# A Mamba block between two graph layers: where the first two chunks' convolutions and heads keep their accumulators, when the second head runs, and when activation tables are called for

## The chip, the cores and the metric

The kernel runs on one core of a Trainium2 chip. The metric is the device time of one execution in microseconds (us); of several executions the median is taken. The engines of a core work at the same time, each through its own queue in order: TensorE (PE in the profile; its weight loads are PEld), VectorE (DVE), ScalarE (ACT), GpSimd (POOL) and SyncE (SP, which here only issues DMA transfers). Matrix products land in PSUM, which this kernel divides into eight banks of 128 x 512 float32; everything else lies in SBUF.

## The reference, cut to what matters

Four graph layers follow each other on 3327 nodes with 256 features, each with a residual sum and a layer norm around it. Layer 1 is the one that the change touches: a graph convolution, then a Mamba block over the nodes as a sequence.

```
h = relu(adj @ x @ gcn_w + gcn_b)
h = (h - mu) * rsqrt(var + eps) * ln_g + ln_b
# _mamba(h):
xz = h @ w_in                      # 256 -> 2 * 512
xc, z = xz[:, :512], xz[:, 512:]
xconv = sum(xpad[k:k + L] * conv_w[:, k] for k in range(4)) + conv_b
u = silu(xconv)
dbc = u @ w_xp                     # 512 -> 16 + 16 + 16
dt = softplus(dbc[:, :16] @ w_dt + b_dt)
B, C = dbc[:, 16:32], dbc[:, 32:]
dA = exp(dt[:, :, None] * A[None]);  dBu = dt[:, :, None] * B[:, None, :] * u[:, :, None]
hst = dA_t * hst + dBu_t           # a scan over the nodes, 16 states a channel
y = (hst @ C_t) + u * D_skip
return (y * silu(z)) @ w_out
```

Softplus is computed as max(v, 0) + log(1 + exp(-|v|)) with a correction for rounding.

## The kernel before

The 3327 nodes are padded to 26 tiles of 128. Layer 0 comes first, TensorE alone being busy. Layer 1 follows, and its sequence is cut into seven **chunks**: one of 256 nodes (tiles 0 and 1), then six of 512 (four tiles each). Layers 2 and 3 come after it and are not touched.

**Graph convolution.** `convolve()` (L308) is a generator that yields after every few matmuls. For each tile it multiplies 26 blocks of the adjacency matrix, fetched in three transfers of up to nine blocks into two buffers (L318, L319), with the features, into `acc`, one half of a PSUM tile `cb` (L313). Then the tile's **evacuation** follows: ACT copies it (L328), PE transposes it into the other half `tp` (L331), ACT copies again (L333), PE multiplies with `gcn_w` into `acc` (L336, L337), and ACT takes relu out of it (L340), which is the last read of `cb`. ACT and POOL then make the layer norm (L298 to L306, L347), PE transposes (L357) and ACT writes the tile into `hT` (L359), the input of Mamba. Each unit of work has a count: 122 a tile (`TILE`), 96 of them for the matmuls of 24 blocks.

**A head** (class `Head`, L460) prepares one chunk: `project(g)` for the four groups g of 128 channels (two matmuls, then on ACT a copy and the first tap, L474 to L477); `taps(g)`, three multiply-adds on DVE (L484); `silu` (ACT); `mixed`, the product with `w_xp` and its copy to `left` (L498 to L500), from which B and C also go to DRAM (L503); `step_size(g)`, a small matmul and two ACT operations (L512 to L514); `exponentials(g)` for two groups at a time (ACT Exp of `e`, then `e1 = 1 + e`); `rounding` (DVE, L526), `logarithms` (ACT Ln of `e1`), `finish` (three DVE operations, L534 to L537; `e1` is then dt, and `du` is dt times u) and `skip` (ACT multiplies u by D_skip). The big temporaries of the heads, `xc`, `left`, `v`, `e`, `e1`, come from `scratch()` (L199), a pool of four buffers of one tile name `t`. `e1` stays in use as dt for the whole chunk.

**The states.** A chunk is worked off in 16 **slots**, one for each state s. In a slot DVE does four scans (L586, one a group) and one product with C (L593, into one of two buffers `hc`), and POOL makes the scan's input for two slots later (`feed`, L580). ACT makes the decays dA (L572) into two PSUM buffers, each released by its scan. PE adds the product, transposed, to the accumulators `y0` to `y3` (`add_up`, L601; one bank for each tile of the chunk). The rows of B and C come by DMA on SP's queue (L569), into three buffers.

**Order.** The main loop runs over all 7 x 16 slots. In slot s of chunk c the steps of the head of chunk c + 1 are put where `plan(c)` says (L246), and convolution units for the chunk after that are spread over the slots: `quota` (L409) levels the counts of `duty` (L390) and adds 96 units (`AHEAD`) at the start. A scheduler then orders the instructions of PE and ACT by priority and by when it thinks operands are there; steps under `tc.high_priority()` go ahead, among them the sums of the first slots (L671: `s == 0 or k < 5`). In the loop (`pinned`) DVE and POOL keep the order in which the program was written, and steps called through `in_turn` (L279: decays, silu, exponentials, logarithms) keep theirs on ACT.

**Before the loop** tiles 0 and 1 are convolved (L635), the first head runs at high priority (L638), and tiles 2 to 5 are convolved (L652).

**PSUM.** The pools of layer 1 hold eight banks: `y0` to `y3`, one for each; `ps`, one for everything else of the heads, gates and residuals; two for dA; and one for `cb`. The first chunk has two tiles, so it uses `y0` and `y1` only, and `y2` and `y3` are first used when the second chunk begins.

Of the kernel before, what the change touches and what calls it, by code (L numbers as in the profile page):

```python
# [9 lines left out]
F32 = mybir.dt.float32  # L10
# [37 lines left out]
def gnn_kernel(ctx: ExitStack, tc: tile.TileContext, n: int, a: dict, out: bass.AP):  # L48
# [109 lines left out]
    with tc.tile_pool(name="l1b", bufs=1) as wpool, tc.tile_pool(name="l1at", bufs=2) as l1at:  # L158
# [33 lines left out]
        with tc.tile_pool(name="l1aw", bufs=1) as cwork, tc.tile_pool(name="l1c", bufs=2) as ch, \  # L192
# [53 lines left out]
            def plan(c):  # L246


                if c == 0:
                    return dict(project={g: (g,) for g in range(NG)}, taps={g + 2: (g,) for g in range(NG)}, gates={6: (0, 1)},  # L250
                                silu=5, mixed=7, sizes={g + 8: (g,) for g in range(NG)}, exps=(11, 12), log=13)
                return dict(project={5: (0, 1), 6: (2, 3)}, taps={7: (0, 1), 8: (2, 3)}, gates={7: (0, 1), 8: (2, 3)},
                            silu=8, mixed=9, sizes={9: (0,), 10: (1, 2), 11: (3,)}, exps=(11, 12), log=13)

# [35 lines left out]
                gps.tensor_scalar(rs, var, EPS, None, op0=ALU.add)  # L290
                gps.tensor_tensor(rs, rs, mhalf[:, :var.shape[1]], op=ALU.pow)

            def back_to_exp():
                in_turn(act.activation, small.tile([P, 1], F32, name="ex"), eps_t, AF.Exp)

            def spread(y, sm, nm, sq):

# [10 lines left out]
            def convolve():  # L308

                rest = []  # L310
                full = 0
                for it in range(nt):
                    cb = cpsum.tile([P, 2, D], F32, name="cb")  # L313
                    acc, tp = cb[:, 0, :], cb[:, 1, :]
                    for j in range(nt):
                        if j % JC == 0:
                            m = min(JC, nt - j)
                            at = l1at.tile([P, JC, P], F32, name="at")  # L318
                            nc.sync.dma_start(at[:, :m, :], a["adjT"][it][:, j:j + m, :])  # L319
                        ten.matmul(acc, at[:, j % JC, :], X0[:, j, :], start=(j == 0), stop=(j == nt - 1))  # L320
                        if j % JM == JM - 1 and j < nt - 1:
                            if rest:
                                step = rest.pop(0)
                                step()
                                full += step is turn
                            yield full, 4 * JM
                    m = cwork.tile([P, D], F32, name="m")
                    act.copy(m, acc)  # L328
                    yield full, 8
                    for k in range(2):  # L330
                        ten.transpose(tp[:, k * P:(k + 1) * P], m[:, k * P:(k + 1) * P], ident)  # L331
                    mt = cwork.tile([P, D], F32, name="m")
                    act.copy(mt, tp)  # L333
                    yield full, 4
                    for k in range(2):
                        ten.matmul(acc, mt[:, k * P:(k + 1) * P], gw[:, k, :], start=(k == 0), stop=False)  # L336
                    ten.matmul(acc, one, gb, start=False, stop=True)  # L337
                    h = cwork.tile([P, D], F32, name="hn")
                    rs, nb, nm, sm, sq = (small.tile([P, 1], F32, name=x) for x in ("rs", "nb", "nm", "sm", "sq"))
                    act.activation(h, acc, AF.Relu, accum_out=sm)  # L340
                    spread(h, sm, nm, sq)

                    def measure(rs=rs, nb=nb, nm=nm, sq=sq):
                        scales(rs, nb, nm, sq)

                    def norm(h=h, rs=rs, nb=nb):
                        turn_or_not = in_turn if pinned else lambda op, *x, **k: op(*x, **k)  # L347
                        turn_or_not(act.activation, h, h, AF.Identity, scale=rs, bias=nb)

                    def turn(it=it, h=h):  # L350
                        c = next(x for x in range(nch) if it * P < ends[x])
                        i = it * P - starts[c]
                        if i == 0:
                            hTs[c] = ch.tile([P, D // P, WC], F32, name="hT", bufs=3)
                        pt = psum.tile([P, WC], F32, name="ps")
                        for k in range(2):
                            ten.transpose(pt[:, k * P:(k + 1) * P], h[:, k * P:(k + 1) * P], ident)  # L357
                        for k in range(2):
                            act.activation(hTs[c][:, k, i:i + P], pt[:, k * P:(k + 1) * P], AF.Identity,  # L359
                                                 scale=g1[:, k:k + 1], bias=b1[:, k:k + 1])  # L360
                    rest = [*2 * [lambda: None], measure, *2 * [lambda: None], norm, lambda: None, turn]
                    if not pinned:
                        for step in (measure, norm, turn):
                            step()
                        rest = []
                        full += 1
                    yield full, 14
                for step in rest:
                    step()
                    full += step is turn  # L370
                    yield full, 0
# [88 lines left out]
            class Head:  # L460
# [4 lines left out]
                def project(self, g):  # L465

                    c, w = self.c, self.w
                    if g == 0:
                        self.xc = scratch()
                        gps.tensor_copy(self.xc[:, :, :3], last)  # L470
                        us[c] = ch.tile([P, NG, WC], F32, name="u", bufs=1)[:, :, :w]
                    ps = psum.tile([P, WC], F32, name="ps")
                    for k in range(2):
                        ten.matmul(ps[:, :w], w_in[:, k, g * P:(g + 1) * P], hTs[c][:, k, :w],  # L474
                                   start=(k == 0), stop=(k == 1))
                    act.copy(self.xc[:, g, 3:3 + w], ps[:, :w])
                    act.activation(us[c][:, g, :], self.xc[:, g, 0:w], AF.Identity, scale=conv_w[:, g, 0:1],  # L477
                                   bias=conv_b[:, g:g + 1])
# [13 lines left out]
                def mixed(self):  # L492

                    c, w = self.c, self.w
                    m = w_sp.shape[2]
                    ps = psum.tile([P, WC], F32, name="ps")
                    for g in range(NG):
                        ten.matmul(ps[:m, :w], w_sp[:, g, :], us[c][:, g, :], start=(g == 0), stop=(g == NG - 1))  # L498
                    self.left = scratch()[:m, 0, :w]
                    act.copy(self.left, ps[:m, :w])  # L500
                    bc = rows_of[c] = l1d.tile([2, DS, w], F32, name=f"bc{c}")
                    for k in range(2):
                        nc.sync.dma_start(bc[k], self.left[32 * k + DTR:32 * k + DTR + DS])  # L503

                def step_size(self, g):

                    w = self.w
                    if g == 0:
                        self.v, self.e = (scratch()[:, :, :w] for _ in range(2))
                    ps = psum.tile([P, WC], F32, name="ps")  # L510
                    k = slice(32 * g, 32 * g + DTR)
                    ten.matmul(ps[:, :w], w_dt[k, :P], self.left[k], start=True, stop=True)  # L512
                    act.activation(self.v[:, g, :], ps[:, :w], AF.Identity, bias=b_dt[:, g:g + 1])
# [63 lines left out]
                in_turn(act.activation, dA, dt[:, g, :], AF.Exp, scale=A[:, g, states[k][1]:states[k][1] + 1])  # L577
                return dA

            def feed(k):  # L580

                du = xs[states[k][0]][1]
                w = du.shape[2]
                gps.tensor_tensor(hs[k % 2][:, :, :w], du, rows[k][:, 0:1, :].to_broadcast([P, NG, w]), op=ALU.mult)

            def scan(k, g, dA):  # L586

# [23 lines left out]
            def gated(c, i):  # L611

                pt = psum.tile([P, NG, P], F32, name="ps")
                for g in range(NG):
                    ten.transpose(pt[:, g, :], szs[c][:, i, g * P:(g + 1) * P], ident)
                gt = tmp.tile([P, NG, P], F32, name="gt", bufs=1)
                act.copy(gt, pt)
                return gt

# [18 lines left out]
            with tc.high_priority():  # L638
                for g in range(NG):
                    first.project(g)  # L640
                    first.taps(g)
                first.silu()
                first.mixed()
                for g in range(NG):
                    first.step_size(g)
                for g in (0, 2):
                    first.exponentials(g)
                first.rounding()
                first.logarithms()
                first.finish()  # L650
                first.skip()
            pump(ends[1] // P)  # L652
            states = [(c, s) for c in range(nch) for s in range(DS)]
            rows = {k: row(k) for k in range(2)}
            for k in range(2):
                feed(k)
            dAs = [decay(0, g) for g in range(2)]
            pinned = True
            added = None
            turned = []  # L660
            for k, (c, s) in enumerate(states):
# [39 lines left out]
                    scales(plus[0], plus[1], plus[2], plus[4])  # L701
                if s == 14:
                    in_turn(act.activation, szs[c], szs[c], AF.Silu)
                    back_to_exp()
                if after:
                    if s == p["silu"]:
                        ahead.silu()
                        back_to_exp()
                    elif s == p["log"]:
                        ahead.logarithms()  # L710
                        back_to_exp()
                    elif s == 15:
                        ahead.skip()
                    if s in p["exps"]:
# [864 lines left out]
```

## Time and profile before

| | us |
|---|---|
| median of three runs (3562.14 to 3568.34) | 3562.71 |
| the profiled execution, whole | 3553.07 |
| its span, first to last instruction | 3551.3 |
| PE, DVE, ACT, POOL busy in the span | 3267.4, 2370.3, 1736.8, 931.8 |
| first matmul of the graph convolution (tile 0) | about 357 |
| first scan of chunk 0 | 428.1 |
| first scan of chunk 1 | 570.3 |
| last product of chunk 6 done | 1403.0 |

How to read the lines: a group of instructions is given as engine, line of the code, operation, output <- input, shape, and count; a bracket at the end says how long the engine was idle before it, and which engine and tile ended that. Lines at L274 are calls through the class that pins the order, and lines at L281 are calls through `in_turn`, so there one goes by the tile's name: `h<-dA` is a scan, `hc` a product, `u<-t` the taps, `dA` a decay, and `t<-t` exponentials or logarithms. A float32 matmul is recorded as two instructions. In a table of stretches of time, each line gives the stretch, its length, and then for each engine the busy time and the number of instructions in it, followed by the granted TensorE clock, the share of DMA time and GB/s.

### The profile page before, as it was taken

The page shows a single profiled execution, that of the slowest core. Times are in us where ns is not written, and L with a number is a line of the kernel's source. Part 1 is how long each engine was busy: PE and PEld are TensorE (multiplying, and loading weights), DVE is VectorE, ACT ScalarE, POOL GpSimd, SP SyncE. Part 2 cuts the span into 40 slices and gives each one's busy share as a digit, 9 for nine tenths or more (in the row PEclk, how much of TensorE's full clock was granted, in tenths as well). Part 3 has the DMA queues.
Part 4 walks back from the last instruction along what each step waited for, and adds up shares of the span by engine and source line. Part 5 has one row for each costly group of instructions (what it writes and reads, how often), then busy time and mean ns, then how long its engine had stood idle before and what let it go on. Part 6 is the DMA issues. An engine that isn't in the chain of part 4 may idle for free. (4 is left out here: it accounts for less than half of the span.)

```text
span 3551.3 us, 43260 instructions
## 1 busy us (share of the span) xinstructions
PE 3267.4 (92%) x15595; PEld 2565.1 (72%) x15595; DVE 2370.3 (67%) x5246; ACT 1736.8 (49%) x2743; POOL 931.8 (26%) x942
## 2 busy tenths in 40 slices
PE   9999898898988866899899999999998999999996
PEld 7888666576666654788768787777775777777775
DVE  1111248999999898777554445454533999999996
ACT  0000446766767764111133333333336788888883
POOL 0000135666665554111100000000001233333332
PEclk9999999899999887999999999999999999999998
DMA  7443334334333221444322121212212112222220
GB/s 246 142 137 104 93 110 112 94 109 118 106 105 99 60 64 44 145 149 147 109 62 64 48 67 49 64 53 59 63 48 75 48 58 67 69 61 69 70 61 20
DMA packets 147577, 307.99 MB, mean 87 GB/s; under 512 B 19570, under 2 KB 64722, under 8 KB 147218
## 3 DMA queue, kind: packets, MB, share of 16 engines
q1 hardware_dynamic: 147346, 305.06, 28.8%
q8 instruction: 126, 2.06, 0.2%
q14 instruction: 105, 0.86, 0.1%
HBM read 294.36 MB, written 10.65 MB: 86 GB/s over the span
## 5 line engine op out<-in xcount | busy, mean ns | idle before, releaser
L274 POOL TENSOR_TENSOR h<-du,row 128x2048 f32<-128x2048 f32 (+1 forms) x110 | 467.7, 4252 | 372.5 <-DVE hc L274 297.5
L274 DVE TENSOR_TENSOR_SCAN h<-dA,carry,h 128x512 f32<-128x512 f32 x384 | 466.1, 1266 | 37.7 <-ACT dA L281 37.5
L281 ACT ACTIVATE dA<-t,A_log 128x512 f32<-128x512 f32 (+1 forms) x448 | 292.5, 658 | 153.7 <-DVE h L274 151.2
L1022 PE MATMUL acc<-F,at 128*128 128x256 f32 x1352 | 354.1, 387 | 1.0 <-ACT q L796 0.6
L1055 PE MATMUL acc<-X,wt 128*128 128x256 f32 x1352 | 345.2, 392 | 10.5 <-ACT wt L1053 10.3
L1055 PE MATMUL acc<-G,wt 128*128 128x256 f32 x1352 | 337.1, 392 | 5.6 <-ACT wt L986 5.1
L320 PE MATMUL cb<-F,at 128*128 128x256 f32 x1352 | 331.0, 395 | 5.1 <-ACT hn L340 5.1
L1055 PEld LDWEIGHTS acc<-X,wt 128*128 128x128 f32 x1352 | 243.8, 190 | 105.8 <-issue 41.3
L120 PE MATMUL acc<-xa,at 128*128 128x257 f32 x1352 | 308.5, 381 | 6.0 <-DMA at<-in_adjT 5.9
L320 PEld LDWEIGHTS cb<-F,at 128*128 128x128 f32 x1352 | 261.0, 199 | 65.4 <-issue 18.9
L1022 PE MATMUL acc<-X,at 128*128 128x256 f32 x1352 | 308.2, 381 | 0.0
L931 PE MATMUL acc<-F,at 128*128 128x257 f32 x1352 | 303.3, 381 | 1.4 <-DMA U<-in_U 1.4
L1055 PEld LDWEIGHTS acc<-G,wt 128*128 128x128 f32 x1352 | 250.7, 193 | 66.0 <-ACT wt L986 35.5
L1067 DVE MAX8 cand<-e 128x8 f32<-128x128 f32 x676 | 142.3, 279 | 228.3 <-ACT e L1008 216.7
L1022 PEld LDWEIGHTS acc<-F,at 128*128 128x128 f32 x1352 | 238.2, 190 | 75.2 <-issue 50.2
L120 PEld LDWEIGHTS acc<-xa,at 128*128 128x128 f32 x1352 | 255.4, 191 | 43.1 <-issue 6.3
L1022 PEld LDWEIGHTS acc<-X,at 128*128 128x128 f32 x1352 | 252.9, 191 | 39.8 <-issue 7.8
L931 PEld LDWEIGHTS acc<-F,at 128*128 128x128 f32 x1352 | 253.2, 190 | 37.0 <-issue 1.6
L605 PE MATMUL y<-ident,hc 128*128 128x128 f32 x1664 | 243.5, 303 | 35.0 <-DVE hc L274 34.8
L605 PEld LDWEIGHTS y<-ident,hc 128*128 128x128 f32 x1664 | 218.8, 158 | 76.8 <-DVE hc L274 51.4
L274 DVE TENSOR_TENSOR hc<-h,row 128x2048 f32<-128x2048 f32 (+1 forms) x112 | 241.0, 2152 | 18.2 <-PE y L605 12.5
L1053 ACT COPY wt<-tp 128x512 f32<-128x512 f32 (+1 forms) x182 | 93.6, 557 | 310.9 <-PE tp L1051 310.6
(324 smaller groups left out, 5199.1 us busy)
## 6 DMA issues: line engine op xcount, KB each, us to landing
at<-in_adjT SPq DMA_DIRECT2D x102, 832.0 KB, 4.5
at<-in_adjT SPq DMA_DIRECT2D x260, 320.0 KB, 3.0
row<-bc SPq DMA_DIRECT2D x96, 512.0 KB, 4.9
at<-in_adjT SPq DMA_DIRECT2D x52, 576.0 KB, 3.9
at<-in_adjT SPq DMA_DIRECT2D x26, 512.0 KB, 3.7
row<-bc SPq DMA_DIRECT2D x16, 256.0 KB, 4.8
xt<-in_xT SPq DMA_DIRECT2D x26, 128.0 KB, 4.0
qd<-q SPq DMA_DIRECT2D x104, 32.0 KB, 1.9
```

The source lines that it names most:

```text
L120: nc.tensor.matmul(acc, at[:, j, :], rhs[:, j0 + j, :], start=(j0 + j == 0), stop=(j0 + j == nt - 1))
L274: return lambda *x, **k: tc.keep_in_program_order(op(*x, **k))
L281: decays.append(op(*x, **k))
L320: ten.matmul(acc, at[:, j % JC, :], X0[:, j, :], start=(j == 0), stop=(j == nt - 1))
L605: ten.matmul(y[:, g * P:(g + 1) * P], h[:, g, i * P:(i + 1) * P], ident, is_transpose=True, start=(first and g == 0), stop=(last and g == ...
L931: nc.tensor.matmul(acc, at[:, j, :], F[:, j0 + j, :], start=(j0 + j == 0), stop=(j0 + j == nt - 1))
L1022: nc.tensor.matmul(acc, at[:, j, :], rhs[:, j0 + j, :], start=(j0 + j == 0), stop=(j0 + j == nt - 1))
L1053: copy(wt[:, :m, :], pt[:, :m, :])
L1055: nc.tensor.matmul(acc, wt[:, j, :], rhs[:, j0 + j, :], start=(j0 + j == 0), stop=(j0 + j == nt - 1))
L1067: nc.vector.max(cand[:, s * 8:(s + 1) * 8], z[:, s * SEG:(s + 1) * SEG])
```

## The change

Six things are edited.

1. `plan(0)`, which places the second head in the slots of chunk 0: projections in slots 1 to 4 in place of 0 to 3, taps in 6 to 9 in place of 2 to 5, gates in 5 in place of 6, silu in 9 (was 5), mixed in 10 (was 7), step sizes two in slot 10 and two in 11 (was one each in 8 to 11).
2. The matmuls of the first head (chunk 0) rotate over `y0`, `y1` and `ps`, those of the second over `y2`, `y3` and `ps`. Later heads still have `ps` alone.
3. The convolutions of tiles 2 to 5 take `y2` and `y3` in turn for `cb`.
4. `left` is no longer a scratch buffer: it shares the single buffer `gt` of the gated outputs. This holds for all heads.
5. In the first head a one-column activation (`table_of`) stands where the next function's table is to be in place: Exp after silu, Ln after the exponentials, Exp after the logarithms.
6. The first head's `skip` is moved behind the first two decays, the first feed is cut into four pieces of one group each, and feeds, decays and skip are at high priority.

```
-                    return dict(project={g: (g,) for g in range(NG)}, taps={g + 2: (g,) for g in range(NG)}, gates={6: (0, 1)},
-                                silu=5, mixed=7, sizes={g + 8: (g,) for g in range(NG)}, exps=(11, 12), log=13)
+                    return dict(project={g + 1: (g,) for g in range(NG)}, taps={g + 6: (g,) for g in range(NG)}, gates={5: (0, 1)},
+                                silu=9, mixed=10, sizes={10: (0, 1), 11: (2, 3)}, exps=(11, 12), log=13)
...
+            def table_of(function):
+                in_turn(act.activation, small.tile([P, 1], F32, name="ex"), eps_t, function)
+
+            banks = {0: ["y0", "y1", "ps"], 1: ["y2", "y3", "ps"]}
+
+            def bank(c):
+
+                if c not in banks:
+                    return psum.tile([P, WC], F32, name="ps")
+                banks[c].append(banks[c].pop(0))
+                x = banks[c][-1]
+                return psum.tile([P, WC], F32, name="ps") if x == "ps" else ypsum.tile([P, DI], F32, name=x)
...
-                    cb = cpsum.tile([P, 2, D], F32, name="cb")
-                    acc, tp = cb[:, 0, :], cb[:, 1, :]
+                    if 1 < it < ends[1] // P:
+                        cb = ypsum.tile([P, DI], F32, name=f"y{2 + it % 2}")
+                    else:
+                        cb = cpsum.tile([P, DI], F32, name="cb")
+                    acc, tp = cb[:, :D], cb[:, D:]
...
-                    ps = psum.tile([P, WC], F32, name="ps")          # in project, mixed, step_size
+                    ps = bank(self.c)
...
-                    self.left = scratch()[:m, 0, :w]
+                    self.left = tmp.tile([P, WC], F32, name="gt", bufs=1)[:m, :w]
...
-            def feed(k):
+            def feed(k, step=NG):
...
-                gps.tensor_tensor(hs[k % 2][:, :, :w], du, rows[k][:, 0:1, :].to_broadcast([P, NG, w]), op=ALU.mult)
+                for g in range(0, NG, step):
+                    gps.tensor_tensor(hs[k % 2][:, g:g + step, :w], du[:, g:g + step, :],
+                                      rows[k][:, 0:1, :].to_broadcast([P, step, w]), op=ALU.mult)
...
                 first.silu()
+                table_of(AF.Exp)
                 first.mixed()
...
                     first.exponentials(g)
+                table_of(AF.Ln)
                 first.rounding()
                 first.logarithms()
+                table_of(AF.Exp)
                 first.finish()
-                first.skip()
...
-            for k in range(2):
-                feed(k)
-            dAs = [decay(0, g) for g in range(2)]
+            with tc.high_priority():
+                feed(0, 1)
+                dAs = [decay(0, g) for g in range(2)]
+                first.skip()
+                feed(1)
```

More of the change, by code (lines that the diff above doesn't have):

```diff
@@ L291, in power @@
                 gps.tensor_tensor(rs, rs, mhalf[:, :var.shape[1]], op=ALU.pow)
-            def back_to_exp():
-                in_turn(act.activation, small.tile([P, 1], F32, name="ex"), eps_t, AF.Exp)
+            def table_of(function):
[7 more added lines that the diff above has]
+                return psum.tile([P, WC], F32, name="ps") if x == "ps" else ypsum.tile([P, DI], F32, name=x)
             def spread(y, sm, nm, sq):
@@ L495, in mixed @@
                     m = w_sp.shape[2]
-                    ps = psum.tile([P, WC], F32, name="ps")
+                    ps = bank(self.c)
                     for g in range(NG):
                         ten.matmul(ps[:m, :w], w_sp[:, g, :], us[c][:, g, :], start=(g == 0), stop=(g == NG - 1))
-                    self.left = scratch()[:m, 0, :w]
+                    self.left = tmp.tile([P, WC], F32, name="gt", bufs=1)[:m, :w]
                     act.copy(self.left, ps[:m, :w])
@@ L509, in step_size @@
                         self.v, self.e = (scratch()[:, :, :w] for _ in range(2))
-                    ps = psum.tile([P, WC], F32, name="ps")
+                    ps = bank(self.c)
                     k = slice(32 * g, 32 * g + DTR)
@@ L615, in gated @@
                     ten.transpose(pt[:, g, :], szs[c][:, i, g * P:(g + 1) * P], ident)
-                gt = tmp.tile([P, NG, P], F32, name="gt", bufs=1)
+                gt = tmp.tile([P, WC], F32, name="gt", bufs=1).rearrange("p (g t) -> p g t", g=NG)
                 act.copy(gt, pt)
@@ L703, in gnn_kernel @@
                     in_turn(act.activation, szs[c], szs[c], AF.Silu)
-                    back_to_exp()
+                    table_of(AF.Exp)
                 if after:
@@ L707, in gnn_kernel @@
                         ahead.silu()
-                        back_to_exp()
+                        table_of(AF.Exp)
                     elif s == p["log"]:
                         ahead.logarithms()
-                        back_to_exp()
+                        table_of(AF.Exp)
                     elif s == 15:
```

## The prediction, made before the changed kernel was run

> **What bounds the kernel now.** First the page's 40 slices, for the stage.
>
> ```profile
> PE   9999898898988866899899999999998999999996
> DVE  1111248999999898777554445454533999999996
> ```
>
> A slice is 88.8 us. Slices 1 to 4 (to 355 us) are layer 0, PE alone. Slices 7 to 16 show DVE at 8 or 9: Mamba. Slice 5 and most of 6 belong to neither: the convolution of tiles 0 to 5, PE not full and DVE nearly idle. The table of stretches, cut at the events that matter, sizes this (columns: stretch, length, busy time and instructions of PE, PEld, DVE, ACT, POOL, clock, DMA share, GB/s).
>
> ```profile
> 383.70:467.30 83.60, 70.13 (x304) 54.60 (x304) 20.59 (x30) 38.04 (x88) 14.34 (x18) 0.94 0.34 98
> 476.00:570.30 94.30, 86.81 (x385) 63.08 (x384) 66.86 (x83) 64.78 (x138) 40.10 (x23) 0.96 0.43 115
> 570.30:1406.50 836.20, 688.92 (x3326) 521.01 (x3325) 778.67 (x586) 554.84 (x1100) 497.50 (x174) 0.89 0.33 91
> ```
>
> From the last matmul of tile 1 to that of tile 5 (first line) PE is the late engine, yet idle for 83.6 - 70.1 = 13.5 us. In chunk 0 (second) PE is busy 92%, DVE 71%. In chunks 1 to 6 (third) DVE is busy 93%: there a DVE stall is time. Third, the timeline of DVE at its long stops.
>
> ```profile
> 437.71 0.66 DVE L274 TENSOR_TENSOR_SCAN h<-dA,h 128x256 f32<-128x256 f32 x1
> 479.40 2.32 DVE L274 SCALAR_TENSOR_TENSOR u<-t,conv_w,u 128x512 f32<-128x512 f32 x3 [41.03 <-issue]
> ...
> 542.34 1.27 DVE L274 TENSOR_TENSOR_SCAN h<-dA,h 128x256 f32<-128x256 f32 x2 [7.86 <-ACT dA L281]
> ```
>
> DVE stands 41 us in slot 2, because `taps(0)` of the second head, pinned there, needs tiles 2 to 5. Then why PE idles, at tile 3:
>
> ```profile
> 417.59 8.46 PE L320 MATMUL cb<-F,at 128*128 128x256 f32 x38
> ...
> 424.51 1.71 ACT L281 ACTIVATE u<-u,D_skip 128x256 f32<-128x256 f32 x4 [3.54 <-DVE du L537]
> 426.23 1.28 ACT L281 ACT_TABLE_LOAD   x1
> 427.52 0.88 ACT L281 ACTIVATE dA<-t,A_log 128x256 f32<-128x256 f32 x2
> 428.82 1.06 ACT L281 ACTIVATE dA<-t,A_log 128x256 f32<-128x256 f32 x2 [0.42 <-DVE h L274]
> 429.81 0.36 ACT L328 COPY m<-cb 128x256 f32<-128x256 f32 x1
> ```
>
> The matmuls end at 426.05; the copy out of the only `cb` stands behind skip, table load and decays until 429.81, and the next tile may not start before relu has read `cb` (435.4). Last, ACT in slot 11 of chunk 3, and the scan that follows:
>
> ```profile
> 949.42 1.04 ACT L281 ACTIVATE t<-t 128x1024 f32<-128x1024 f32 x1
> 950.58 0.69 ACT L513 ACTIVATE t<-ps,b_dt 128x512 f32<-128x512 f32 x1
> 951.17 0.68 ACT L514 ACTIVATE t<-ps,b_dt 128x512 f32<-128x512 f32 x1
> 953.53 1.06 ACT L281 ACTIVATE t<-t 128x1024 f32<-128x1024 f32 x1 [1.68 <-PE ps L512]
> ...
> 957.12 1.28 DVE L274 TENSOR_TENSOR_SCAN h<-dA,carry,h 128x512 f32<-128x512 f32 x1 [4.37 <-ACT dA L281]
> ```
>
> Exp of `e` runs at 949.42; the next step, `e1 = 1 + e`, needs only that, yet waits for PE's L512, the last `step_size`. What they share is a buffer: with dt, `left`, `v`, `e` held, the four scratch buffers are full, so `e1` gets `left`'s when the last `step_size` has read it. Decays queue behind on ACT, DVE stands 4.37 us. The 7.86 us at 542.34 have the same cause (`e1` at 539.45, released by L512).
>
> **What the skill says.** The Trainium skill's "PSUM — Partial Sum Buffer", Specifications, gives 8 banks of 2 KiB a partition; all are allotted here (4 + 1 + 2 + 1), so overlap must come from idle `y` banks. Its "Perfetto Trace Analysis", Tensor Engine Instruction, says that ACT, DVE and GpSimd are strict FIFO; the copy at 429.81 agrees. Its "ScalarE: Activation LUTs", What ACT_TABLE_LOAD costs, puts a load at 1283 ns plus a drain of 1380; the trace has 1.28 us, and the decay starts 1.29 us after the load's start: no drain behind it.
>
> **The change, part by part.**
>
> *Tiles 2 to 5 in y2 and y3.* The next tile's matmuls no longer await relu. At most the 13.5 us come back. Against it: two more sums at high priority (products 2 and 3; eight transposes are 0.87 us in a run), 1.75; and the adjacency. A block of nine is 18 records at 0.213 us (469 in 100 us of layer 0), 3.8 us; a transfer takes 3.8 us (median to landing in this stretch) and needs the buffer of the block before last, so PE runs just as fast as data comes. Waits of 0.16 to 0.33 us show now; the rows of slots 2 to 7 (six transfers of 256 KB, 4.8 us) move in too, on the same SP queue, where an adjacency transfer behind a row waits for that row's buffer. Bounds 0 to 5 us; I take 1.75. Gain 10: tile 5 ends at 457.3, not 467.3.
>
> *First head: three banks, tables early, skip later, feed in pieces.* Step sizes lose the wait for `ps` (408.5 to 413.2 now; four of 0.84 us on ACT back to back would end at 409), Ln starts after rounding rather than at 419.56, the first decays no longer follow skip (1.71) and a load (1.28): the first scan comes near 419, not 428.1. No loads are added (four before, four after), three activations of 0.20 us. A POOL product of 256 columns has no row: between 0.20 (12 columns) and 2.36 us (1024), 0.6 by share. I cost all this at **nothing**: slots 0 to 5 (3.7 us each: four scans 2.5, product 1.22) end near 442, and DVE then waits until 473. That 31 us wait covers the 9 us and the delays that skip brings to slot 0 (1.2). Without it the 9 us would count. On POOL six feeds of 2.36 us come earlier; a norm of tile 5 behind one loses up to 2.4, inside the 4.4 below.
>
> *Second head later.* Slot 0 gets 96 + 27 = 123 units, by the code's own levelling: all of tile 6, ahead of `project(0)` in slot 1. PE: 457.3 + 11.1 (52 records) + 1.7 (tile 5's evacuation) = 470.1. Tile 5's chain to `hT` takes 8.4 us (467.3 to 475.7 now), ready at 465.7, so tile 6 costs 4.4. With 1.75 matmul, 0.3, and 1.4 on ACT, `taps(0)` starts at 473.5, not 479.4; but DVE then stands in slot 6, not 2.
>
> *From there to chunk 1.* DVE: taps 4 x 2.3, nine slots of scans x 2.5, ten products x 1.22, rounding 2.3, finish 6.9: 53.1. Stalls: silu 2.5, logarithm 2.0, skip and gates 2.1, as now; the 7.86 goes, but step sizes in slots 10 and 11 stand right ahead of exponentials in 11 and 12, an estimate of 4 + 3 (PE 3.6 for mixed, then 2 x (1.1 + 1.4) and 2.1 for a pair of exponentials, against two slots of 3.7); sums that are late on PE, 4. Total 70.7: 544.2. PE: 86.8 busy now, less tile 6's other 38 records (8.1) and two sums (1.75), is 77.0; of 7.5 idle I keep 4.5: 470.1 + 81.5 = 551.6. PE is later, so chunk 1 starts at **551**, not 570.3: gain 19, bounds 10 (all idle time kept, 5 us of rows) and 26 (the DVE sum).
>
> *left in gt.* `e1` then finds `xc`'s buffer, free since the taps. `gt`'s other user is done by slot 4. DVE's waits for dA in slots 11 and 12 are 2.96, 3.96, 4.66, 4.67, 2.51 us in chunks 1 to 5, 18.8 together. The last step sizes on ACT (1.3) and other heads' norms can still stand ahead of a decay, and chunk 5's stall has little of this wait: I take 13, bounds 5 and 17. Behind DVE the next limit is PE, 689 busy of 836 us: slack enough.
>
> **Sum.** 19 + 13 = 32. Units of convolution through slot 15 are 501 before 504, so the later slots find PE in the same place, and layers 2 and 3 move as a block. Profiled execution 3553.07 - 32 = 3521; the median was 9.6 above it, so 3562.7 - 32 = **3531**.
>
> **Rivals.** (a) Only chunk 0 gains: PE's order of step sizes, on the single `ps`, is the real cause of the stalls in slot 11. For it: ACT also waits for `ps` there. Against: `e1` itself waits at L512. 3562.7 - 19 = 3544. (b) Transfers pace tiles 2 to 5: tile 5 ends at 467.3 as now, `project(0)` at 480.1, chunk 1 at 561.6: 9 + 13, 3541. (c) PE isn't the limit in chunk 0 and little stall is left in slot 11: 26 + 16, 3521. (d) **Slower: a ring of in-order waits in slots 6 to 12.** The sum of product 4 isn't at high priority (k < 5), so it stands on PE behind the projections; product 6 needs its buffer; decays behind that hold ACT, and ACT holds the next projection's copy. Then slots 6 to 9 run serially: 1.9 + 1.4 + 2.3 + 1.2 + 0.9 + 2.5 + 0.9 + 2.0 (19 units) = 13.1 in place of 6.1, and silu, two loads, mixed, four step sizes and exponentials (1.9 + 2.6 + 3.6 + 0.6 + 10 + 4.2 = 22.9) stand whole in place of 9.5: 41 us, chunk 1 at 592, less 13: 3572. It decides from 32 us lost. Against it: the scheduler fills PE with what is ready (14 records of tile 6 precede `project(0)` now). (e) No effect: a new order of PE and ACT gives back what is won, within 0.2%.
>
> **Chances.** Forecast 0.60, (a) 0.14, (b) 0.08, (c) 0.07, (d) 0.06, (e) 0.05. About 0.2% (7 us) is what a measurement can tell from no change. Faster 0.89, same 0.05, slower 0.06. The range takes in (a) to (c) and the bounds of the unknown terms, 12 to 49 us of gain: 3514 to 3551; (d), (e) stay out.
>
> **What would show it.** First scan near 419; no DVE gap in slots 0 to 5, then one of some 30 us ended by `u<-t`; tile 5's last matmul near 457, `taps(0)` near 473, chunk 1's first scan near 551, PE over 93% busy before it; `e1` no longer released by PE at L512 and stalls of dA in slots 11 and 12 of chunks 1 to 5 under 6 us in sum. I am wrong if chunk 1 starts after 565 or the span from there to the end of Mamba stays at 836.

## The result, and the profile after

| us | before | after |
|---|---|---|
| median (lowest to highest), five runs each | 3562.14 (3556.85 to 3568.34) | 3542.16 (3538.27 to 3545.77) |
| ratio, 95% interval | | 0.9944 (0.9929 to 0.9958) |
| profiled execution, whole (span) | 3553.07 (3551.3) | 3542.27 (3540.5) |
| first scan of chunk 0 | 428.1 | 419.0 |
| `taps(0)` of the second head | 479.4 | 495.0 |
| first scan of chunk 1 | 570.3 | 567.1 |
| from there to the end of chunk 6's last product | 832.7 | 819.6 |
| from the end of that product to the end of the span | 2148.3 | 2153.9 |

The changed kernel is 20 us faster; 31.7 were forecast. The two profiled executions are only 10.8 us apart, because the one of the kernel before was 9 us under its median. A second profile of the kernel before (the last experiment) has 572.2 for chunk 1's first scan and 837.8 for chunks 1 to 6. Against the mean of its two profiles (571.3 and 835.3), chunk 0 gave 4.2 us and chunks 1 to 6 gave 15.7. That the two add up to 19.9, the difference of the medians, is in part chance: behind the last product the changed kernel took 2.8 us longer than that mean, and the eight runs below whose chunks 1 to 6 are written as in the changed kernel (all but left_only, left_back, ahead_later and before_again) took 820.9 to 825.5 us there, so that 10 to 14 us is the safer figure. By stage, then, the forecast of 19 + 13 had its first term far too large and its second nearly right.

The page's 40 slices of DVE, after:

```profile
DVE  1111248999999997777454545454433999999996
```

Slices 8 to 15 of DVE are all at 9 (slice 14 was at 8), and in slice 16 Mamba ends earlier: chunks 1 to 6 are denser. Slices this wide can't show what became of chunk 0. The table of stretches, cut at the new events (same columns as before):

```profile
383.70:458.60 74.90, 65.64 (x288) 51.88 (x288) 21.23 (x30) 38.10 (x91) 15.01 (x21) 0.95 0.37 110
458.60:495.02 36.42, 33.97 (x157) 24.91 (x156) 14.69 (x21) 15.32 (x40) 11.05 (x10) 1.00 0.37 102
495.02:567.05 72.03, 64.08 (x277) 46.60 (x276) 51.66 (x63) 52.64 (x109) 28.25 (x17) 0.86 0.40 108
567.05:1390.10 823.05, 672.63 (x3323) 507.45 (x3322) 778.78 (x586) 553.92 (x1100) 483.57 (x174) 0.91 0.33 93
```

The first line is tiles 2 to 5: done at 458.6, 8.7 us before the old 467.3 and near the forecast 457.3. The third, from `taps(0)` to chunk 1, took 72.0 us where 77.5 were forecast. The loss lies in the second: from tile 5's end to `taps(0)` 36.4 us went by, forecast 16.2. In the fourth DVE has the 778.8 us of work that it had before, in 823.1 us in place of 836.2.

DVE's timeline shows two stops, in slots 2 and 5, where the forecast had a single one, in slot 6, ahead of the taps:

```profile
460.85 1.23 DVE L274 TENSOR_TENSOR hc<-h,row 128x1024 f32<-128x1024 f32 x1 [30.30 <-PE y L620]
...
469.03 1.23 DVE L274 TENSOR_TENSOR hc<-h,row 128x1024 f32<-128x1024 f32 x1
488.86 2.51 DVE L274 TENSOR_TENSOR_SCAN h<-dA,h 128x256 f32<-128x256 f32 x4 [18.60 <-POOL h L274]
...
495.02 2.30 DVE L274 SCALAR_TENSOR_TENSOR u<-t,conv_w,u 128x512 f32<-128x512 f32 x3
```

Product 2 waits 30.3 us for a sum on PE (L620 is `add_up`), and slot 5's scans wait 18.6 us for their feed on POOL. `taps(0)` itself waits for nothing: it stands behind them. PE's timeline gives the cause of the first stop.

```profile
443.60 0.27 PE L620 MATMUL y<-ident,u 128*128 128x128 f32 x1
...
458.47 0.38 PE L620 MATMUL y<-ident,u 128*128 128x128 f32 x2
458.68 1.04 PE L620 MATMUL y<-ident,hc 128*128 128x128 f32 x8
...
473.81 1.02 PE L487 MATMUL y<-hT,w_in 128*128 128x512 f32 x2
476.66 3.73 PE L333 MATMUL cb<-F,at 128*128 128x256 f32 x16 [1.84 <-DMA at<-in_adjT]
480.23 1.02 PE L487 MATMUL y<-hT,w_in 128*128 128x512 f32 x2
```

The sum of u, which starts the accumulators (`y<-ident,u`), has no high priority, and the program has it behind tiles 2 to 5. The scheduler put its pieces into the ends of tiles 3, 4 and 5; the sums of products 0 and 1, at high priority themselves, add to the same accumulators and stand behind it until 458.68. `hc` has two buffers, so product 2 waits. (In the kernel before DVE stopped for the taps ahead of product 2, so that this didn't show.) The rest of u's sum and those of products 0 to 3 then run behind tile 5, and the two matmuls of `project(0)` are split by 16 records of tile 6, which wait for their adjacency. POOL's timeline gives the cause of the second stop.

```profile
485.42 0.19 POOL L274 TENSOR_SCALAR rs<-sq 128x1 f32<-128x1 f32 x1 [18.20 <-ACT m L310]
485.69 0.55 POOL L274 TENSOR_TENSOR rs<-rs,mhalf 128x1 f32<-128x1 f32 x1
486.32 0.19 POOL L274 TENSOR_TENSOR nb<-nm,rs 128x1 f32<-128x1 f32 x1
486.46 4.67 POOL L274 TENSOR_TENSOR h<-du,row 128x1024 f32<-128x1024 f32 x2
```

The feed of slot 5 needs the buffer that product 3 has read at 465.8 (464.58 and 1.22). But POOL keeps the order of the program, and slot 0 now writes out all of tile 6, so that the **scales** of tile 6's norm are written ahead of that feed. They need tile 6, which PE finishes after 480. Three instructions of 0.93 us together keep POOL from the feed for 19 us.

What was to be seen of a better overlap is there: the copy out of tile 3's accumulator (L341, once L328) waits for nothing but its matmuls.

```profile
422.08 0.37 ACT L341 COPY m<-y 128x256 f32<-128x256 f32 x1 [0.33 <-PE y L333]
```

And of `left`, in chunk 3, ACT and then DVE:

```profile
952.69 1.05 ACT L281 ACTIVATE t<-t 128x1024 f32<-128x1024 f32 x1
...
953.99 1.05 ACT L281 ACTIVATE t<-t 128x1024 f32<-128x1024 f32 x1
```

```profile
947.95 1.28 DVE L274 TENSOR_TENSOR_SCAN h<-dA,carry,h 128x512 f32<-128x512 f32 x1 [0.92 <-ACT dA L281]
```

`e1` at 953.99 has no bracket: the wait for PE's last `step_size` is gone, and the scan that stood 4.37 us stands 0.92.

### The profile page after: what moved, and what is told of

Read it like the earlier page. It is cut to its first block, busy times and chain, and to the rows that moved or that the text cites. A ratio compares the mean times of both kernels' runs of the same rounds, so it can differ in the third digit from the quotient of the medians.

```text
span 3540.5 us, 43253 instructions
## 1 busy us (share of the span) xinstructions
PE 3248.9 (92%) x15595; PEld 2550.5 (72%) x15595; DVE 2370.3 (67%) x5246; ACT 1736.5 (49%) x2746; POOL 919.0 (26%) x945
## 5 line engine op out<-in xcount | busy, mean ns | idle before, releaser
L274 DVE TENSOR_TENSOR_SCAN h<-dA,carry,h 128x512 f32<-128x512 f32 x384 | 466.1, 1265 | 24.2 <-ACT dA L281 23.9
L333 PE MATMUL cb<-F,at 128*128 128x256 f32 x1144 | 281.6, 396 | 5.2 <-ACT hn L353 3.4
L620 PE MATMUL y<-ident,hc 128*128 128x128 f32 x1664 | 233.6, 295 | 39.3 <-DVE hc L274 39.2
L620 PEld LDWEIGHTS y<-ident,hc 128*128 128x128 f32 x1664 | 209.2, 153 | 80.3 <-DVE hc L274 52.2
L333 PEld LDWEIGHTS cb<-F,at 128*128 128x128 f32 x1144 | 222.1, 200 | 56.7 <-issue 16.0
```

The source lines that it names most:

```text
L274: return lambda *x, **k: tc.keep_in_program_order(op(*x, **k))
L620: ten.matmul(y[:, g * P:(g + 1) * P], h[:, g, i * P:(i + 1) * P], ident, is_transpose=True, start=(first and g == 0), stop=(last and g == ...
```

## The experiments

The theory was: `left` in `gt` gives its part alone; in chunk 0 the gain is held up by the **order** in which each engine takes its work (sums of u, then tile 6's scales and norm), not by the amount of it. The rival: PE's **work** bounds chunk 0 whatever the order. Every time below is a median, every ratio against the kernel before on the same chip.

### left in gt alone, and all but that

left_only is the kernel before with edit 4 only; left_back is the changed kernel with edit 4 undone:

```
-                    self.left = tmp.tile([P, WC], F32, name="gt", bufs=1)[:m, :w]
+                    self.left = scratch()[:m, 0, :w]
```

> The kernel before with only the fourth edit: left in gt's buffer in place of a scratch buffer. Theory (e1 waited for left's buffer): the decay stalls in slots 11 and 12 of chunks 1 to 5 shrink from 18.8 us to about 6, and the 7.9 us of chunk 0 goes too; from chunk 1's first scan to chunk 6's last product 820 us in place of 832.7; total 13 to 19 us below the kernel before, about 3547. Rival (the order of the step sizes on PE and the single ps make the stalls): the stalls stay within 3 us of 18.8, and the time within 4 us of 3562.

Measured: 3545.83 us, ratio 0.9960 (0.9946 to 0.9975). Chunks 1 to 6 took 824.3 us, 11 less than the mean of the two profiles of before. Chunk 1 started at 569.9, as before: the 7.86 us stop in slot 12 of chunk 0 fell to 1.16, as expected, but slot 13 then took 3.10 us (1.15 before), and in this profile tile 5 was done only at 470.9. In chunk 3 of its ACT timeline the wait is gone with this edit and nothing else:

```profile
951.53 1.05 ACT L281 ACTIVATE t<-t 128x1024 f32<-128x1024 f32 x1
...
953.58 0.67 ACT L513 ACTIVATE t<-ps,b_dt 128x512 f32<-128x512 f32 x1
```

`e1` (951.53) runs without a bracket, and the last `step_size` on ACT (953.58) comes after it.

> The changed kernel with left back in a scratch buffer: the chunk 0 edits alone. Theory: from chunk 1's first scan to chunk 6's last product again about 832 us, and e1 in chunk 0 waits again for the last step size, so chunk 1 starts at 567 or some us later; total about 3558 to 3566, no different from the kernel before within the measurement. Rival (the chunk 0 edits carry the gain): 3545 to 3550.

Measured: 3548.74 us, ratio 0.9963 (0.9949 to 0.9978). Chunks 1 to 6 took 832.6 us, 13 more than in the changed kernel, with the 4.38 us stall of chunk 3 back, and `e1` again released by PE's small matmul after 1.68 us. Chunk 1 started at 567.6, as in the changed kernel. Edit 4 is thus worth 11 to 13 us by stage in both directions (7 to 12 if left_back is held against the eight runs named in the section on the result), and the other five edits 4 us in chunk 0. The granted clock doesn't explain it: over chunks 1 to 6 it was 0.89 here and 0.89 in first_plain, which has edit 4 and took 825.5 us. The whole time, though, came out in the range that was expected of the rival: 14 us under before, of which the trace has 6.4 in Mamba (3.7 and 2.7, against the mean of the two profiles) and most of the rest in layers 2 and 3, which no edit touches. (The two ways of counting don't meet: by the medians edit 4 is worth 16.8 us in left_only and 6.6 in left_back. What speaks for 11 to 13 is the wait of `e1` and the stall behind it, gone where the edit is made and back where it is undone.) From the last residual to the end of the span the profiles of all these kernels lie between 2127.7 and 2135.0 us with no relation to the edits; what moves that is open.

### What stops DVE in chunk 0

Four kernels take away one wait after the other. u_high puts the sum of u at high priority in chunk 0:

```
-                    add_up(ys[c], us[c], first=True)
+                    with tc.high_priority() if not c else nullcontext():
+                        add_up(ys[c], us[c], first=True)
```

> The changed kernel, with the sum of u into y in slot 0 of chunk 0 at high priority. Theory (two causes in a row hold DVE): the 30 us wait of product 2 for the sum goes, slots 2 to 4 are done by about 442, but slot 5 still waits for its feed, which stands on POOL behind the scales of tile 6 (near 485), so taps of group 0 start at about 491 in place of 495, chunk 1 at about 563 in place of 567. Rival (the late sum alone made the loss): taps at 475 to 482, chunk 1 at 550 to 556.

Measured: 3543.76 us, 0.9945 (0.9930 to 0.9959). The 30 us stop at product 2 is gone, and slot 5 waits 44.44 us for POOL in its place; `taps(0)` 494.2, chunk 1 at 569.2. The first stop was covered by the second. Chunk 1 came 6 us later than expected, for high priority has a price: the sums now stand ahead of the convolution on PE, and tile 5's last matmul ends at 465.1 in place of 458.6. In every later run with this edit it lies between 463.4 and 464.1.

u_free6 has this edit, and takes tile 6's scales out of the fixed order (`nc.gpsimd` in place of the pinning `gps`):

```
-                        scales(rs, nb, nm, sq)
+                        scales(rs, nb, nm, sq, nc.gpsimd if it == ends[1] // P else gps)
```

> As the run before, and the scales of tile 6 are not bound to the written order on POOL. Theory: slots 0 to 5 are done by about 446, DVE then waits for the projection, taps of group 0 start at about 480, chunk 1's first scan comes at about 552 in place of 567, total 3527 (15 us below the changed kernel). Rival (PE sets chunk 0's end in any order): taps start at 480 but chunk 1's first scan comes after 563.

Measured: 3542.07 us, 0.9938 (0.9926 to 0.9951). Slot 5 still waits 44.26 us for POOL, and `taps(0)` is at 492.9. The edit didn't reach the wait: on POOL the feed (484.32) still stands right behind these scales (from 483.28 on), so it decides nothing on the theory.

u_late6 writes tile 6's scales three steps and its norm one step later in the program, behind the next tile's first units; u_late6_sums puts the sums of products 4 to 6 at high priority too (`k < 8`; in slot k the sum is that of product k - 1):

```
                     rest = [*2 * [lambda: None], measure, *2 * [lambda: None], norm, lambda: None, turn]
+                    if it == ends[1] // P:
+                        rest = [*5 * [lambda: None], measure, norm, turn]
...
-                    with tc.high_priority() if s == 0 or k < 5 else nullcontext():
+                    with tc.high_priority() if s == 0 or k < 8 else nullcontext():
```

> The changed kernel, with the sum of u at high priority, and the scales of tile 6 written three steps later, in slot 4 in place of slot 2, so that the feeds of slots 5 and 6 stand ahead of them on POOL. Theory (those scales held slot 5): DVE does slots 0 to 5 and the scans of slot 6 before 450, taps of group 0 start as soon as u is there, near 482, not 494; but product 6 then waits for the sum of product 4, which PE has behind the projections (near 497), so chunk 1's first scan stays near 565 to 568. Rival 1 (POOL's order was the whole loss): chunk 1 at 555 to 558. Rival 2 (something else holds slot 5): taps stay at 492 to 495.

Measured: 3539.46 us, 0.9936 (0.9921 to 0.9951); `taps(0)` 490.8, chunk 1 at 564.8. The wait for POOL has become one for ACT: slot 5's last two scans stand 41.91 us for their decays.

> As the run before, and the sums of products 4 to 6 at high priority too. Theory (a ring of in-order waits, one behind the other, with PE not yet the limit): taps near 482, no wait at product 6, chunk 1's first scan near 557, 10 us ahead of the changed kernel, total about 3532. Rival (PE is the limit of chunk 0 whatever the order): chunk 1 stays at 564 or later though DVE waits less at product 6.

Measured: 3541.58 us, 0.9937 (0.9924 to 0.9951); `taps(0)` 490.7, chunk 1 at 567.6. The same two scans stand 41.76 us. On ACT the norm of tile 6, called through `in_turn`, runs at 484.77 and the decays at 485.27, right behind it. Each removal showed another hold at the same place with the same root, tile 6 written ahead of slot 5, and none moved the time by more than its interval. By itself this would also fit the rival.

### Parts of the change that were costed

first_plain undoes edits 5 and 6: no tables ahead, skip and feeds as before.

> The changed kernel without the table calls and with feeds, decays and skip of the first head as before (edits 5 and 6 undone). Theory (covered by DVE's wait for the sum behind tile 5): the first scan comes 6 to 9 us later, near 427, but taps and chunk 1's first scan stay within 2 us of 495 and 567; total within 3 us of the changed kernel. Rival (the first head's time counts): chunk 1 at 573 to 576.

Measured: 3539.20 us, 0.9937 (0.9922 to 0.9952). The first scan comes at 423.0, 4 us later than with the edits, and chunk 1 at 563.2, 4 us earlier. The two edits gain nothing in time; "nothing" was their price in the forecast. That they cost 4 us isn't shown: tile 5 was done 4.6 us earlier here (454.0), but 2.4 us of that are the same 284 instructions of PE from tile 1's end on, busy 62.4 us in place of 64.8 at a granted clock of 1.00 in place of 0.95.

one_cb undoes edit 3: tiles 2 to 5 share the single `cb` again.

```
-                    if 1 < it < ends[1] // P:
-                        cb = ypsum.tile([P, DI], F32, name=f"y{2 + it % 2}")
-                    else:
-                        cb = cpsum.tile([P, DI], F32, name="cb")
+                    cb = cpsum.tile([P, DI], F32, name="cb")
```

> The changed kernel with tiles 2 to 5 in the single cb (edit 3 undone). Theory (the overlap of evacuation and matmuls brings tile 5 forward by some 8 us): tile 5's last matmul near 467 in place of 458.5, taps near 503, chunk 1's first scan near 575, total 3550. Rival (what the overlap wins is lost again in waits behind it): taps and chunk 1 within 2 us of the changed kernel's.

Measured: 3551.52 us, 0.9969 (0.9956 to 0.9983). Tile 5's last matmul came 12 us later (470.5), chunk 1 10 us later (577.3), and the time is 9.4 us longer than the changed kernel's. The overlap of the evacuations is worth what the forecast gave it, 10 us; what is more, without it the other edits in chunk 0 are a loss (577.3 against 571.3).

### Order or work

tile6_late takes the 96 units ahead away from slots 0 to 4, so that tile 6 is written out bit by bit behind the projections. ahead_later takes them away from all of chunk 0. ahead_10 gives them back in slot 10. All three have the edits of u_high and u_late6_sums for the sums.

```
-                return TILE * starts[n] // P + sum(shares[n][:k - due(n - 2) + 1]) + AHEAD - taken
+                return TILE * starts[n] // P + sum(shares[n][:k - due(n - 2) + 1]) + AHEAD * (k > 4) - taken
```

(`k > 15` in ahead_later, `k > 9` in ahead_10.)

> The changed kernel, with the sums of u in chunk 0 and those of products 5 and 6 at high priority too, and without the 96 units ahead in slots 0 to 4: tile 6 is convolved behind the projections, its norm behind slot 5, and the 96 units come in slot 5. Whole work is done. If it is the order of tile 6's norm ahead of slot 5 that held chunk 0 (the scales on POOL, or the norm on ACT), no DVE stop of 18 to 44 us stands at slot 5, taps(0) starts near 472, and chunk 1 at 553 to 557, about 10 us before the changed kernel's: 3529 to 3535. If PE's work bounds chunk 0 whatever its order, taps come early but chunk 1 still starts at 563 to 568 and the time stays at 3539 to 3545.

Measured: 3543.44 us, 0.9951 (0.9935 to 0.9967); `taps(0)` 495.0, chunk 1 at 569.3. Its time looked like the rival's, but the trace says that the hold had only moved by a slot. ACT and DVE:

```profile
492.86 0.60 ACT L281 ACTIVATE hn<-hn,nb,rs 128x256 f32<-128x256 f32 x1 [0.74 <-POOL nb L274]
493.36 0.86 ACT L281 ACTIVATE dA<-t,A_log 128x256 f32<-128x256 f32 x2
```

```profile
493.85 1.27 DVE L274 TENSOR_TENSOR_SCAN h<-dA,h 128x256 f32<-128x256 f32 x2 [46.25 <-ACT dA L281]
495.04 2.30 DVE L274 SCALAR_TENSOR_TENSOR u<-t,conv_w,u 128x512 f32<-128x512 f32 x3
```

With the units back in slot 5, tile 6's norm was written there, ahead of slot 6's last two decays. DVE stands 46 us in slot 6 for an activation of 0.60 us, and `taps(0)`, whose operands had been there since about 475 (ACT wrote u at 474.28), starts behind it. So this run didn't test what it was to test.

> As the run before, but the 96 units ahead come only in slot 0 of chunk 1, so that chunk 0 has about one tile's convolution less on PE (some 10 us). Whole work is done. If PE's work bounds chunk 0, chunk 1 starts some 8 to 10 us before the run before's; if order bounds it, both start within 2 us of each other. Whether it is kept: chunk 1 has to do the tile instead, beside DVE work with PE 84% busy, so I expect 0 to 5 us of it back in stalls there.

Measured: 3526.59 us, 0.9904 (0.9882 to 0.9926), an interval apart from the changed kernel's. `taps(0)` 475.3, chunk 1 at 552.0, chunks 1 to 6 821.5 us: nothing is given back there. Order and work are both changed here, and the next run parts them.

> As the run before, but the 96 units come back in slot 10 of chunk 0: through slot 9 each engine has the order of the run before, and by slot 15 chunk 0 has the changed kernel's full 501 units. Whole work is done. It parts the two things that the run before changed together. If the gain of 15 us came from the order alone (tile 6's norm behind the taps), chunk 1 starts within 3 us of that run's 552 and the time is 3526 to 3531. If it came from the tile's 10 us of PE work that left chunk 0, taps(0) stays at 475 but chunk 1 starts at 560 to 564 and the time is 3534 to 3540. Half and half would be 555 to 559, 3530 to 3535.

Measured: 3532.30 us, 0.9914 (0.9898 to 0.9931). DVE at the taps, and PE ahead of them:

```profile
474.56 2.33 DVE L274 SCALAR_TENSOR_TENSOR u<-t,conv_w,u 128x512 f32<-128x512 f32 x3 [26.40 <-ACT u L490]
```

```profile
456.32 7.09 PE L333 MATMUL y<-F,at 128*128 128x256 f32 x32
...
471.19 1.88 PE L487 MATMUL y<-hT,w_in 128*128 128x512 f32 x4
```

DVE's stops are now those that the forecast described: slots 0 to 5 and slot 6's scans without one beyond 2.1 us, then a single one ended by the taps' own operand, 20.5 us earlier than in the changed kernel. But the forecast's sum for PE didn't come true with it. Tile 5's last matmul ends at 463.4, 6.1 us after the forecast, since the sums at high priority take 8.5 us of PE ahead of it (0.7 in the changed kernel); and of tile 6's 52 records only 22 stand ahead of `project(0)` (471.19), where the forecast had all. The two errors cancel, so that `taps(0)` at 474.6, near the 473.5 of the forecast, is luck. From tile 5's end to chunk 1 it took 93.0 us (forecast 93.7), and PE was busy for 87.5 of them, so that another order behind tile 5 has little more to win.

Chunk 1 starts at 556.5. Of the 15.0 us between the changed kernel (567.05) and ahead_later (552.04), the new order (with the sums' priority, which alone gave nothing in u_high) gives 10.6; the other 4.4 come with the 96 units. Expected were 555 to 559 if both count. These are single profiles, and the two of the kernel before differ by 2 us in this mark, so the proportion is rough; the medians, 9.9 and 5.7 us, agree. What lies behind each part is less clear. The stretch from tile 1's end to chunk 1, in the changed kernel and in ahead_10:

```profile
384.56:567.05 182.49, 162.83 (x713) 122.81 (x714) 87.58 (x112) 106.05 (x239) 54.31 (x47) 0.93 0.38 108
383.70:556.45 172.75, 157.81 (x712) 119.53 (x712) 88.62 (x112) 106.65 (x239) 56.25 (x47) 0.96 0.39 114
```

PE has the same work in both, and of the 9.7 us between them 4.7 are less idle time; the other 5.0 are less busy time, at a clock of 0.96 in place of 0.93. Whether the better clock follows from the order or came by chance was not tested. Nor are the 4.4 us shown to be PE's work. The 96 units are 11.7 us of its busy time (157.81 against 146.15 in ahead_later), but they also bring the norm of one more tile, and in ahead_10 a tile's norm stands on ACT ahead of slot 11's decays, as tile 6's stood ahead of slot 5's. ACT and DVE in ahead_10:

```profile
511.19 0.60 ACT L281 ACTIVATE hn<-hn,nb,rs 128x256 f32<-128x256 f32 x1 [1.22 <-POOL nb L274]
```

```profile
512.18 1.27 DVE L274 TENSOR_TENSOR_SCAN h<-dA,h 128x256 f32<-128x256 f32 x2 [5.28 <-ACT dA L281]
```

In ahead_later the same two scans wait 0.29 us (and those of slot 12 wait 11.65, against 6.24 here). So the same work in another order is 10 us faster, with the clock's part in that open, and how much PE's work holds back stays open too.

### The kernel before once more

before_again is the kernel before, unchanged.

> The kernel before once more, for a second profile of it. Its first profiled execution was 9 us below its median, so that its marks may flatter it. If the difference lies in chunk 0 or in the slots after it, the changed kernel's gain there is larger than the two profiles show; if it lies outside (layers 0, 2 and 3), the gains by stage stand. I expect chunk 1's first scan at 570 to 572 and 832 to 836 us from there to the end of Mamba, and the rest of any difference in layers 2 and 3.

Measured: 3562.03 us, 0.9999 (0.9988 to 1.0010). Its profiled execution took 3565.76 us, 12.7 more than the first one: 2.0 of it before chunk 1 starts, 5.1 in chunks 1 to 6 (the waits for decays there grew by 3.9) and 5.0 behind the last residual. So the first profile flattered the kernel before inside Mamba too, against what was expected, and gains by stage are better taken from the mean of both.

ahead_later beats both kernels: 15.6 us under the changed one, and 35 under the kernel before.

## Why the prediction was right in sign and too large

- **Tiles 2 to 5 in y2 and y3: right.** Forecast 457.3, trace 458.6; one_cb gives the 10 us back.
- **First head earlier, at no gain: right.** First scan 419.0, forecast "near 419"; first_plain without edits 5 and 6 loses nothing.
- **"Slots 0 to 5 end near 442": wrong, and with it the next step.** I counted the sums of products 2 and 3 as more work on PE, but not that all products' sums need the sum of u first, which has no priority. Product 2 ended at 462. This hold was covered by the next one (u_high).
- **`taps(0)` at 473.5: the step that failed; 495.0.** It has two parts. The operand itself was there at 482.9 (end of L490), 9.4 us late: behind tile 5, PE made the sums of u and of products 0 to 3 (38 records, 4.9 us) where I had put 1.75 ahead of its end, split `project(0)` by tile 6, and waited 1.84 us for the adjacency. The other 12.2 us are tile 6's scales ahead of slot 5's feed: slot 5 starts at 488.86, and its scans, a product and slot 6's scans (2.5 + 1.2 + 2.5) precede the taps. I had written that all of tile 6 is issued in slot 0, and costed its matmuls, but not its scales and norm, which stand on POOL and ACT ahead of the feeds and decays of slot 5. ahead_10, with these behind the taps, has them at 474.6 and chunk 1 at 556.5, near the forecast of 473.5 and 551, but the first of these by luck (see there).
- **From the taps to chunk 1, 77.5 us: nearly right.** 72.0 in the changed kernel, 76.8 in ahead_later and 81.9 in ahead_10. The stalls for step sizes, estimated at 4 + 3 us, were 7.42 and 1.93 in the trace, both in slot 12. That PE is the later engine holds in part at most: with the 96 units gone, 11.7 us of PE time, chunk 1 came 4.4 earlier, and not all of that need be PE's work.
- **left in gt, 13 us: right in size.** 13 by left_back, 11 by left_only. But the stalls in slots 11 and 12 of chunks 1 to 5 fell from 18.8 to 7.8 us, not below 6, and slots 14 and 15 gave 2.3 more; the total of waits for decays in chunks 1 to 6 fell by 13.6 (37.5 to 23.9; 41.4 in the second profile of before, 27 to 30 in the eight later runs). What is left is, for example, 0.92 + 0.48 + 0.98 us in chunk 3.
- **The rivals.** The measured 3542 lies between (a) at 3544 and (b) at 3541, but by neither mechanism: chunk 0 lost most of its gain where (a) has it keep all, and transfers didn't pace tiles 2 to 5. The nearest is the kind of hold in (d), instructions in order behind a late one; I looked for it in slots 6 to 12 and among the sums of PE, and it sat in slot 5, on POOL and ACT, for 12 us and not 41.
- **My tests.** Chunk 1 started after 565, which was named as a sign of being wrong, and it was one: the chunk 0 part was wrong. The stretch behind it fell from 836 to 823.

## What to carry to other kernels

When work is written earlier in a program whose queues keep that order, list all that it issues, down to three one-column operations of its norm: each stands ahead of what comes later on its engine until its own inputs are there, however short it is. After taking such a hold away, look for the next one at the same place before concluding that the work itself is the bound; tile6_late gave the rival's time by the theory's mechanism. What is put at high priority pushes back what it overtakes: the sums cost tile 5 some 5 to 6 us. And take two profiles of the kernel before when the expected gain is under one per cent.

## What the runs showed beyond that

The granted TensorE clock in chunk 0 was lower in the changed kernel, 0.80 between 520 and 540 us and 0.84 between 540 and 560, where it was 1.00 before, though PE was not busier there (17.94 and 14.70 us, 18.77 and 16.98 before).

```profile
520.00:540.00 20.00, 17.94 (x65) 10.42 (x64) 9.39 (x13) 15.52 (x38) 5.46 (x3) 0.80 0.31 99
```

The kernel before has its low clock earlier (0.83 and 0.91 from 400 to 440). No run here was made to find what sets it, so a few us between two stages of different clock can't be put down to an edit by one profile alone.
